# A graph layer on one core: node normalisation moved to ScalarE and h split in PSUM, with another order of issue at the head

## The chip, the core and the metric

The kernel runs on one core of one Trainium2 chip. The metric is the device time of one execution in microseconds: for the kernel before it is 5291.49 us, the median of three runs from 5287.43 to 5294.71.

Engines are called by the profile's names: PE (TensorE matmuls; PEld its weight loads), DVE (VectorE), ACT (ScalarE), POOL (GpSimd) and SP (SyncE, which here only issues DMAs). Each engine works through its own queue in order.

## What is computed

One message passing layer with 12500 nodes of 128 features and 412500 edges, of which the destinations are sorted:

```python
h = jnp.maximum(_layernorm(x, axis=-1), 0.0)
h = h @ W_in2f                                              # per node
Wij = ssp(f_ij @ W_f1 + b_f1) @ W_f2 + b_f2                 # per edge, from 20 numbers
x_ij = h[idx_j] * (Wij * rcut_ij[:, None])                  # per edge
agg = jax.ops.segment_sum(x_ij, idx_i, num_segments=12500)  # idx_i = src, idx_j = dst
out = x + ssp(agg @ W_o1 + b_o1) @ W_o2 + b_o2
```

`ssp(x)` is softplus(x) - log 2; `_layernorm` subtracts the mean of a row and divides by the root of its variance plus 1e-5. All arrays are float32.

## The kernel before

**Nodes.** The nodes are taken in 25 quads of up to four tiles of 128 (`QT` = 4, `NQ` = 25; the last quad has two tiles). `make_h(q)` is a generator: each `yield` ends a stage, and the caller decides when the next stage is issued. The stages are: load `xb`; mean and variance on DVE (`bn_stats`, `bn_aggr`) and `rs`, the reciprocal root, as exp(-0.5 ln(v)) on ACT; a correction step for `rs` on DVE, and on DVE the normalised `xb` = (x - mean) rs (L354); transposes on PE into PSUM (`xps`) and their relu on ACT (`xT`); the product with `win` on PE into PSUM (`hps`) and its rounding to bf16 on ACT (`hb[..., 0, :]`, L367); the rest `left` = hps - hb0 on DVE (L370), and its rounding on ACT (L371); the third part on DVE (L373), and the stores of the three bf16 parts into HBM on SP (L379, L388). `h3_t` is a list of overlapping tables of h, one for each neighbourhood of nodes, so that the rows for a chunk of sorted edges lie in one table.

**Edges.** They are taken in 806 chunks of 512 (`CH`), four chunks to a `Group`. For each chunk:
- `rows`: SP reads a start row from `shifts` and asks for 32 rows of h (`near`).
- `hidden`, `hidden_log`, `hidden_end`, for two chunks at a time: PE makes `z` (PSUM), ACT takes abs, exp and ln (L700, L701, L703), DVE adds (`r`, L709).
- `window`: DVE makes the one-hot `at` from `rel`; `pick`: PE multiplies it with `near` into `picked` (PSUM); `picked`: ACT scales it by the edge weight into `hg` (L822, four instructions).
- `bias`: ACT fills `v` in PSUM with the bias of the second layer (L793); `value`: PE adds r times `wf2` to it (L801).
- `message`: DVE copies the place (L829) and multiplies `v` with `hg` (`o`, L830), and POOL scatters its four tiles into HBM with four indirect DMAs (L834), each to the row in `slot`.
- `columns` (`edges` and `starts`), `blocks`, `rank` and `rank_end` find that row: for each edge the block of 128 source nodes, and by a running count in the PSUM bank `free` the next free slot of that block. `edges` and `starts` work for up to eight groups at once.

`step(k)` issues in this order: groups and rows ahead of time, the message of chunk k, the rest of the last rank, `picked` and `value` of chunk k+1, `pick` and `bias` of chunk k+2, the window of k+3, the end of the hidden layer, blocks, ranks, logs, and `hidden` of chunk k+4. `part(name, upto, make)` issues all chunks up to `upto` that are not yet issued.

**Around it.** The slots are cleared by SP from a tile `zero` (L1218); `zeros` spreads these DMAs over the steps, from step `t0` on. In every step from the sixth on `side()` advances the quads 2 to 24 by one stage, a new quad each nine steps, so the node work ends at step 213 (1352 us); it also checks the ranges of `dst`. After each of seven segments of chunks, `Collect` reads the slots back, compares their places (`to`) and sums them on PE into `agg`; the first of these starts at 2223 us. From step `XK` = 300 on `x_ahead` loads 14 quads of x early and adds the output bias `bo2` to them on DVE (`x_bias`, L426); others follow at the end on POOL. `finish` applies the last two layers.

**Tiles in PSUM.** `acc` (one bank) is shared by `xps`, `hps` and the sums, `v` (three banks) by `v` and `picked`, `z` has two, `free` one, and `count_ps`, which holds the numbers 0 to 127 in each partition, is a tile of its own in a last one.

**The head.** Before the first step the calls at the end of the kernel issue the first stages of quad 0 between the first chunk's work by hand: `h` is the list of the generators of quads 0 and 1, `next(h[0])` advances quad 0.

Of the kernel before, what the change touches and what calls it, by code (L numbers as in the profile page):

```python
# [9 lines left out]
F32 = mybir.dt.float32  # L10
# [7 lines left out]
P = 128  # L18
# [25 lines left out]
def gnn_kernel(  # L44
# [76 lines left out]
    def spread(t, n):  # L121
        return t[:, None, :].to_broadcast([t.shape[0], n, P])
# [204 lines left out]
    def make_h(q, psum):  # L327
# [9 lines left out]
        for i in range(n):  # L337
# [7 lines left out]

        ve = ln.tile([P, QT], F32, name="ve")
        nc.vector.tensor_scalar(ve[:, :n], mv[:, :n, 1], EPS, -0.5, op0=ALU.add, op1=ALU.mult)
        r2 = ln.tile([P, QT], F32, name="r2")
# [3 lines left out]
                                       op0=ALU.add, op1=ALU.mult)  # L352
        for i in range(n):
            nc.vector.tensor_scalar(xb[:, i, :], xb[:, i, :], mv[:, i, 0:1], rs[:, i:i + 1],  # L354
                                    op0=ALU.subtract, op1=ALU.mult)
# [10 lines left out]
        hb = ln.tile([P, QT, 3, P], BF16, name="hb")  # L366
        nc.scalar.activation(hb[:, :n, 0, :], hps[:, :n, :], AF.Copy)  # L367
        yield
        left = ln.tile([P, QT, P], F32, name="left")
        nc.vector.tensor_sub(left[:, :n, :], hps[:, :n, :], hb[:, :n, 0, :])  # L370
        nc.scalar.activation(hb[:, :n, 1, :], left[:, :n, :], AF.Copy)  # L371
        yield
        nc.vector.tensor_sub(hb[:, :n, 2, :], left[:, :n, :], hb[:, :n, 1, :])  # L373
        for (b, rows), table in zip(tables, h3_t):
# [47 lines left out]

    def x_bias(xo, pieces, engine=nc.vector):
        for p, cs, rows in pieces:
            xi = xo[:p, cs, :]
            engine.tensor_add(xi, xi, spread(bo2[:p, :], xi.shape[1]))  # L426

# [110 lines left out]
    with tc.tile_pool(name="edge", bufs=2) as edge, tc.tile_pool(  # L538
# [10 lines left out]

        count_ps = state_ps.tile([P, P], F32, name="count_ps")  # L550

# [42 lines left out]
        class Group:  # L594
# [45 lines left out]
            def columns(self):  # L640
                self.edges()
                self.starts()

            def edges(self):
                if len(self.cols) == 3:
                    w, src_i, _ = self.cols
                    part = edge.tile([P, SB * TG], I32, name="part")
                    nc.vector.tensor_scalar(part[:, :w], src_i[:, :w], 7, None,
                                            op0=ALU.logical_shift_right)
                    blk = edge.tile([P, SB * TG], F32, name="blk")  # L650
                    nc.vector.tensor_copy(blk[:, :w], part[:, :w])
                    nc.vector.tensor_scalar(src_i[:, :w], src_i[:, :w], P - 1, None,
                                            op0=ALU.bitwise_and)
                    place = edge.tile([P, SB * TG], F32, name="place")
                    nc.vector.tensor_copy(place[:, :w], src_i[:, :w])
                    self.cols += [blk, place]
                self.rcut, self.blk, self.place = (t[:, self.at] for t in self.cols[2:5])

            def starts(self):
                if len(self.cols) == 5:  # L660
                    w, blk = self.cols[0], self.cols[3]
                    seg = self.seg
# [15 lines left out]
                    for t, half in ((1, -1.0), (2, 0.0)):  # L678
# [3 lines left out]
                                            seg.T * P - 1.0, None, op0=ALU.add)  # L682
                    self.cols += [start]
                self.start = self.cols[5][:, self.at]

# [103 lines left out]
            def bias(self, c):  # L789


                v = psum.tile([P, QT, P], F32, name="v", bufs=3)
                nc.scalar.activation(v, spread(bf12, QT), AF.Copy)  # L793
                return v
# [184 lines left out]
        def group(j):  # L979
            if j not in groups and j < NG:  # L980
                groups[j] = Group(j)
# [11 lines left out]
        def step(k, units=()):  # L993
# [12 lines left out]
            def message(k):  # L1006
# [96 lines left out]

        def x_ahead(homes, engine):

            pending = []
            for q, xo in homes:
                n = min(QT, NTILE - q * QT)
                pieces = x_pieces(q * QT, n)
                x_load(xo, pieces)  # L1110
                xs[q] = xo
                pending.append((xo, pieces))
                yield
                yield
                if len(pending) > 2:
                    x_bias(*pending.pop(0), engine)
            for w in pending:
                yield
                x_bias(*w, engine)

# [30 lines left out]
        def rest():  # L1151
# [15 lines left out]
            yield from ranges(psum)  # L1167
            late_biases(psum)

        def side():  # L1170
# [12 lines left out]
        with tc.manual_schedule():  # L1183
# [157 lines left out]
```

## Time and profile before

| | |
|---|---|
| median of three runs | 5291.49 us |
| the profiled run | 5291.49 us |
| its span, first to last instruction | 5289.7 us |
| first message `o` starts | 22.27 us |
| first scatter starts | 23.26 us |
| last stage of the last quad (stores on SP) | 1349 to 1352 us |
| early additions to x (L426) | 1920.8 to 2061.7 us, 14 of 677 ns (median) |
| first read of slots | 2223.2 us |
| last scatter starts | 5158.9 us |
| PE clock granted, mean | 0.760 |

The profile is one execution. A group's line has the source line, engine, operation, what it writes and reads with their shapes, how often (x); then the busy time in us, the mean in ns of one, and how long the engine idled just before, with what ended that. Busy time of a group counts overlapping instructions of one engine once. In a timeline the first two numbers are start and duration in us; rows that follow each other are merged (x4), and brackets give the idle time before and what ended it. "issue" is a wait that the profile can't explain, "remote" one ended by a semaphore of which the profile has no instruction. SPq rows are DMA issues on SP's queue. A table of stretches gives for each the busy time and count, the granted clock, the DMA engines' busy share and GB/s.

### The profile page before, as it was taken

How to read it: one execution, taken by the hardware profiler on the slowest of the kernel's cores; microseconds unless marked ns; L12 is line 12 of the kernel's file. 1: busy time of each engine (PE TensorE's matmuls, PEld its weight loads, DVE VectorE, ACT ScalarE, POOL GpSimd, SP SyncE). 2: the span in 40 equal slices, each digit the busy share in tenths (PEclk: the TensorE clock that was granted, in tenths of full speed). 3: DMA queues.
4: the chain of work that ended last, by engine and by line, in shares of the span. 5: the costliest groups of instructions: out<-in, count | busy, mean ns of one | idle time of the engine just before them, and what ended most of it. 6: DMA issues, size and time to landing. Idle time of an engine off the chain costs nothing. (4 is left out here: it accounts for less than half of the span.)

```text
span 5289.7 us, 74340 instructions
## 1 busy us (share of the span) xinstructions
PE 3721.0 (70%) x21594; PEld 2858.0 (54%) x21594; DVE 3142.9 (59%) x7101; ACT 2785.5 (53%) x5466; POOL 3137.3 (59%) x3292
## 2 busy tenths in 40 slices
PE   5565655555665555688888887777787787777778
PEld 4344434334443333466666666666666666666667
DVE  5555555554444454566666666566666666666667
ACT  5555555555555555555555555455554454554443
POOL 5666666656666666666665565555555565555552
PEclk7666666666666666688888878888888888888889
DMA  4545445444333334465666555556555665565547
GB/s 139 155 135 158 143 137 150 126 138 132 109 101 99 97 111 135 132 181 179 179 180 206 175 167 171 153 169 206 173 165 168 191 191 150 170 192 160 152 134 195
DMA packets 515221, 820.65 MB, mean 155 GB/s; under 512 B 177188, under 2 KB 312728, under 8 KB 514812
## 3 DMA queue, kind: packets, MB, share of 16 engines
q1 hardware_dynamic: 411212, 602.55, 40.3%
q0 software_dynamic: 103168, 213.15, 12.1%
q8 instruction: 180, 2.95, 0.2%
q14 instruction: 229, 1.88, 0.1%
q10 hardware_dynamic: 432, 0.13, 0.0%
HBM read 419.75 MB, written 395.69 MB: 154 GB/s over the span
## 5 line engine op out<-in xcount | busy, mean ns | idle before, releaser
L834 POOL DMA_INDIRECT slots<-o,slot x3224 | 3099.7, 961 | 2056.3 <-DVE o L830 1161.4
L822 ACT ACTIVATE hg<-picked,rcut 128x128 f32<-128x128 f32 x3224 | 912.3, 365 | 1400.0 <-remote 716.5
L907 PEld LDWEIGHTS acc<-to,m 128*128 128x128 f32 x8152 | 1210.2, 230 | 478.2 <-issue 338.1
L907 PE MATMUL acc<-to,m 128*128 128x128 f32 x8152 | 1303.7, 321 | 209.0 <-issue 130.4
L801 PEld LDWEIGHTS v<-wf,r 128*128 128x128 f32 x6448 | 1082.8, 249 | 384.7 <-issue 264.4
L801 PE MATMUL v<-wf,r 128*128 128x128 f32 x6448 | 1176.6, 338 | 120.9 <-issue 75.4
L830 DVE TENSOR_TENSOR o<-v,hg 128x512 f32<-128x512 f32 x806 | 552.4, 685 | 967.4 <-remote 469.5
L691 PE MATMUL z<-f,wf 20*128 20x512 f32 x1612 | 635.3, 861 | 468.8 <-DVE r L709 264.4
L886 DVE TENSOR_TENSOR to<-count_ps,m 128x640 f32<-128x640 f32 (+3 forms) x793 | 637.3, 826 | 283.2 <-remote 98.3
L738 DVE TENSOR_REDUCE top<-free 128x4 f32<-128x392 f32 x806 | 448.2, 556 | 446.9 <-remote 286.1
L793 ACT ACTIVATE v<-bf 128x512 f32<-128x512 f32 x806 | 486.0, 603 | 419.3 <-DVE o L830 244.5
L812 PE MATMUL picked<-near,at 96*128 96x128 bf16 x3224 | 389.7, 255 | 394.4 <-DVE o L830 280.0
L709 DVE SCALAR_TENSOR_TENSOR r<-z,nbf,a 128x1024 f32<-128x1024 f32 x403 | 513.9, 1275 | 95.6 <-issue 50.5
L700 ACT ACTIVATE a<-z,bf 128x1024 f32<-128x1024 f32 x403 | 445.0, 1104 | 221.4 <-remote 79.1
L766 PE MATMUL free<-inb,rest_of 128*128 128x392 f16 x806 | 328.0, 407 | 332.0 <-issue 214.7
L812 PEld LDWEIGHTS <-at 96*128 96x128 bf16 x3224 | 309.5, 117 | 453.0 <-issue 428.1
L691 PEld LDWEIGHTS z<-f,wf 20*128 20x128 f32 x1612 | 157.8, 233 | 679.9 <-DVE r L709 353.9
L703 ACT ACTIVATE a<-a,half 128x1024 f32<-128x1024 f32 x403 | 462.7, 1148 | 13.1
L714 DVE TENSOR_TENSOR inb<-count_ps,blk 128x392 f16<-128x392 f32 x806 | 445.3, 553 | 0.0
L701 ACT ACTIVATE a<-a 128x1024 f32<-128x1024 f32 x403 | 425.9, 1057 | 12.8
L733 PE MATMUL free<-inb,after 128*128 128x392 f16 x806 | 329.4, 409 | 9.6 <-issue 6.6
L785 DVE TENSOR_SCALAR at<-rel,prow 96x512 bf16<-96x512 bf16 x806 | 283.5, 352 | 0.0
(113 smaller groups left out, 1227.9 us busy)
## 6 DMA issues: line engine op xcount, KB each, us to landing
m<-slots SPq DMA_DIRECT2D x307, 387.0 KB
m<-slots SPq DMA_DIRECT2D x278, 322.5 KB
rel<-rel_d SPq DMA_DIRECT2D x202, 384.0 KB
slots<-o,slot POOLq DMA_INDIRECT x3224
m<-slots SPq DMA_DIRECT2D x193, 258.0 KB
slots<-zero SPq DMA_DIRECT2D x96, 387.0 KB
f<-in_f_t SPq DMA_DIRECT2D x404, 80.0 KB
slots<-zero SPq DMA_DIRECT2D x58, 516.0 KB
```

The lines of the kernel that those rows point to most:

```text
L691: mm = nc.tensor.matmul(z[:, k, :], wf1[rows, :], self.f[rows, :], start=True, stop=True)
L703: nc.scalar.activation(a, a, AF.Ln, bias=half, scale=0.5)
L709: nc.vector.scalar_tensor_tensor(r, z, nbf1, a, op0=ALU.max, op1=ALU.add)
L738: nc.vector.tensor_reduce(self.top[:, c * QT:(c + 1) * QT], free_v, axis=mybir.AxisListType.X, op=ALU.max)
L793: nc.scalar.activation(v, spread(bf12, QT), AF.Copy)
L801: mm = nc.tensor.matmul(v[:, i, :], r[:, i * P:(i + 1) * P], wf2, start=False, stop=True, skip_group_check=True)
L812: mm = nc.tensor.matmul(ps[:, i, :], at[:, i * P:(i + 1) * P], near, start=i == 0, stop=i == QT - 1, skip_group_check=True)
L822: nc.scalar.activation(hg[:, i, :], ps[:, i, :], AF.Copy, scale=self.rcut[:, j:j + 1])
L830: nc.vector.tensor_mul(o[:, :, :P], v, hg)
L834: put = nc.gpsimd.indirect_dma_start(out=views[j % VIEWS], out_offset=bass.IndirectOffsetOnAxis(ap=self.slot[:, j:j + 1], axis=0), in_=o[: ...
L886: nc.vector.tensor_tensor(to[:, :n, :], count_ps[:, None, :].to_broadcast([P, n, P]), m[:, :n, P:].to_broadcast([P, n, P]), op=ALU.is_equal)
L907: nc.tensor.matmul(self.acc[b // QT][:, i, :], m[:, j, :P], to[:, j, :], start=t == 0, stop=t == self.seg.tiles(b) - 1)
```

## The change

For quads 2 to 24 the mean is subtracted on ACT, with the negative mean `nm` as bias; the factor `rs`, which is positive and so passes through the relu, is applied when h is rounded: four instructions on ACT in place of one, and four on DVE in place of one. For all quads the rest is kept in `hps` in PSUM, so the tile `left` is gone as a step of the split. The early additions to x read the bias from PSUM (`bo2_ps`, beside `count_ps` in one tile), filled once by ACT. The bias of the first two chunks is made by PE with a one-row matmul. The order at the head differs: `edges` and `starts` are one function, the calls before the first step stand in another order, rows for the first steps are asked for later, `hidden` of chunk 2 is issued a step earlier, the message of chunk 1 stands at its place in step 1 instead of in step 0, and the clears begin at step 0 instead of 8.

```diff
 def make_h(q, psum):
         ve = ln.tile([P, QT], F32, name="ve")
+        if q > 1:
+            nm = ln.tile([P, QT], F32, name="nm")
+            nc.vector.tensor_scalar(nm[:, :n], mv[:, :n, 0], -1.0, None, op0=ALU.mult)
+            for i in range(n):
+                nc.scalar.activation(xb[:, i, :], xb[:, i, :], AF.Identity, bias=nm[:, i:i + 1])
...
-        for i in range(n):
+        for i in range(n if q < 2 else 0):
             nc.vector.tensor_scalar(xb[:, i, :], xb[:, i, :], mv[:, i, 0:1], rs[:, i:i + 1],
                                     op0=ALU.subtract, op1=ALU.mult)
...
-        nc.scalar.activation(hb[:, :n, 0, :], hps[:, :n, :], AF.Copy)
+        if q < 2:
+            nc.scalar.activation(hb[:, :n, 0, :], hps[:, :n, :], AF.Copy)
+            yield
+            nc.vector.tensor_sub(hps[:, :n, :], hps[:, :n, :], hb[:, :n, 0, :])
+        else:
+            for i in range(n):
+                nc.scalar.activation(hb[:, i, 0, :], hps[:, i, :], AF.Copy, scale=rs[:, i:i + 1])
+            yield
+            for i in range(n):
+                nc.vector.scalar_tensor_tensor(hps[:, i, :], hps[:, i, :], rs[:, i:i + 1],
+                                               hb[:, i, 0, :], op0=ALU.mult, op1=ALU.subtract)
+        nc.scalar.activation(hb[:, :n, 1, :], hps[:, :n, :], AF.Copy)
         yield
-        left = ln.tile([P, QT, P], F32, name="left")
-        nc.vector.tensor_sub(left[:, :n, :], hps[:, :n, :], hb[:, :n, 0, :])
-        nc.scalar.activation(hb[:, :n, 1, :], left[:, :n, :], AF.Copy)
-        yield
-        nc.vector.tensor_sub(hb[:, :n, 2, :], left[:, :n, :], hb[:, :n, 1, :])
+        nc.vector.tensor_sub(hb[:, :n, 2, :], hps[:, :n, :], hb[:, :n, 1, :])
...
-        count_ps = state_ps.tile([P, P], F32, name="count_ps")
+        numbers = state_ps.tile([P, CH], F32, name="numbers")
+        count_ps, bo2_ps = numbers[:, :P], numbers[:, P:2 * P]
...
 class Group, bias(self, c):
-                nc.scalar.activation(v, spread(bf12, QT), AF.Copy)
+                if self.g * NCHUNK + c < 2:
+                    nc.tensor.matmul(v.rearrange("p t f -> p (t f)"),
+                                     ones[0:1, :].to_broadcast([1, P]), spread(bf12[0:1, :], QT),
+                                     start=True, stop=False, skip_group_check=True)
+                else:
+                    nc.scalar.activation(v, spread(bf12, QT), AF.Copy)
...
 def step(k, units=()):
-            for j in range(max(groups) + 1, min(k + LG, 2 * k + 8) // NCHUNK + 1):
-                group(j)
-            part("rows", min(k + LW, 2 * k + 5, NEXT if k < NEXT - 3 else NCH), rows)
+            group((k + LG) // NCHUNK)
+            part("rows", min(k + LW, 2 * k + 3, NEXT if k < NEXT - 3 else NCH), rows)
...
-            if k in vs:
-                message(k)
+            if has(k):
+                g, c = of(k)
+                g.message(c, vs.pop(k), hgs.pop(k))
...
-            if k:
-                part("end", min(k + LZ - 2, made.get("log", -1)), pairs(hidden_end))
+            part("end", min(k + LZ - 2, made.get("log", -1)), pairs(hidden_end))
...
-            if not k:
-                message(1)
-                part("end", made["log"] - 1, pairs(hidden_end))
-            part("hidden", k + LZ if k > -2 else 1, pairs(hidden))
+            part("hidden", k + LZ, pairs(hidden))
...
-        t0, i = 8, 0
+        t0, i = 0, 0
...
             late_biases(psum)
+            nc.scalar.activation(bo2_ps, bo2, AF.Copy)
...
             next(h[0])
-            groups[0].edges()
+            part("hidden", 0, hidden)
+            part("blocks", 0, blocks)
             next(h[0])
-            part("hidden", 0, hidden)
-            groups[0].blocks(0)
-            made["blocks"] = 0
+            ready = ranks(0)
+            next(ready)
             next(h[0])
             part("log", 0, hidden_log)
-            next(h[0])
-            part("rows", 3, rows)
-            biases(psum)
-            bs[0] = groups[0].bias(0)
-            ready = ranks(0)
-            next(ready)
-            groups[0].starts()
-            part("end", 0, hidden_end)
-            part("window", 0, window)
             next(ready, None)
             made["rank"] = 0
+            next(h[0])
+            part("rows", 1, rows)
+            biases(psum)
+            part("end", 0, hidden_end)
+            bs[0] = groups[0].bias(0)
             group(1)
             aside = side()
-            x_early = x_ahead(early_homes(), nc.vector)
-            x_late = x_ahead(late_homes(), nc.gpsimd)
+            x_early = x_ahead(early_homes(), nc.vector, bo2_ps)
+            x_late = x_ahead(late_homes(), nc.gpsimd, bo2)
```

`x_bias` and `x_ahead` take the bias to add as a new argument; `blocks` calls `columns`, which does the work of `edges` and `starts` in one.

More of the change, by code (lines that the diff above doesn't have):

```diff
@@ L421, in x_load, with x_bias @@
             nc.sync.dma_start(xo[:p, cs, :], x[rows, :].rearrange("(c p) f -> p c f", p=p))
-    def x_bias(xo, pieces, engine=nc.vector):
+    def x_bias(xo, pieces, engine=nc.vector, b=bo2):
         for p, cs, rows in pieces:
             xi = xo[:p, cs, :]
-            engine.tensor_add(xi, xi, spread(bo2[:p, :], xi.shape[1]))
+            engine.tensor_add(xi, xi, spread(b[:p, :], xi.shape[1]))
     def finish(t0, n, sT, quad, psum, z, xo=None, bank=("v", 3)):
@@ L640, in columns @@
             def columns(self):
-                self.edges()
-                self.starts()
-            def edges(self):
                 if len(self.cols) == 3:
@@ L655, in edges @@
                     nc.vector.tensor_copy(place[:, :w], src_i[:, :w])
[L656 to L661, printed above, removed]
                     seg = self.seg
@@ L682, in starts @@
                                             seg.T * P - 1.0, None, op0=ALU.add)
-                    self.cols += [start]
-                self.start = self.cols[5][:, self.at]
+                    self.cols += [blk, place, start]
+                self.rcut, self.blk, self.place, self.start = (t[:, self.at] for t in self.cols[2:])
             def hidden(self, c):
@@ L998, in has @@
                 return 0 <= j < NCH
-            for j in range(max(groups) + 1, min(k + LG, 2 * k + 8) // NCHUNK + 1):
-                group(j)
-            part("rows", min(k + LW, 2 * k + 5, NEXT if k < NEXT - 3 else NCH), rows)
+            group((k + LG) // NCHUNK)
+            part("rows", min(k + LW, 2 * k + 3, NEXT if k < NEXT - 3 else NCH), rows)
             for c, u in units:
                 c.load(u + AHEAD)
-            def message(k):
+            if has(k):
                 g, c = of(k)
                 g.message(c, vs.pop(k), hgs.pop(k))
-            if k in vs:
-                message(k)
             for r in tops:
@@ L1102, in gnn_kernel, with x_ahead @@
                     break
-        def x_ahead(homes, engine):
+        def x_ahead(homes, engine, b):
             pending = []
@@ L1115, in x_ahead @@
                 if len(pending) > 2:
-                    x_bias(*pending.pop(0), engine)
+                    x_bias(*pending.pop(0), engine, b)
             for w in pending:
                 yield
-                x_bias(*w, engine)
+                x_bias(*w, engine, b)
         def as_quad(t):
```

## The prediction

> **What bounds the kernel now.** I read the page first, then the rate of scatters by stretch of time, then the timeline of one stretch, then the groups of the node work, and last the timeline of the head.
>
> ```profile
> span 5289.7 us, 74340 instructions
> PE 3721.0 (70%) x21594; PEld 2858.0 (54%) x21594; DVE 3142.9 (59%) x7101; ACT 2785.5 (53%) x5466; POOL 3137.3 (59%) x3292
> ...
> L834 POOL DMA_INDIRECT slots<-o,slot x3224 | 3099.7, 961 | 2056.3 <-DVE o L830 1161.4
> ```
>
> No engine is full. POOL's 3224 scatters are four to each of 806 chunks; one takes 961 ns and the next starts 0.30 us after it, so POOL alone would need 4 x 1.26 = 5.04 us for a chunk, 4065 us in all. It also stands idle 1161 us for the messages `o`. So the chain that makes a message (PE, ACT, DVE) falls behind POOL again and again. How much the node work, which the change edits, has to do with that is read from the rate with it (until 1350 us) and without it (after):
>
> ```profile
> 100.00:700.00 600.00, 376.24 (x391) 0.65 0.49 148
> 700.00:1300.00 600.00, 368.67 (x383) 0.66 0.46 135
> 1400.00:1700.00 300.00, 190.60 (x199) 0.63 0.37 102
> 1700.00:2000.00 300.00, 192.19 (x198) 0.64 0.38 109
> ```
>
> The columns are the stretch, its length, POOL's busy time and scatters, clock, DMA share, GB/s. With node work: 774 scatters in 1200 us, 6.20 us a chunk; without: 397 in 600 us, 6.05. A quad of nodes is spread over nine steps, so it costs 9 x 0.156 = 1.41 us now, and the 23 quads from the third on cost 32 us together. That is the size of the stake: whatever is done to this work, little more than 32 us can be won.
>
> ```profile
> 613.73 1.12 ACT L822 ACTIVATE hg<-picked,rcut 128x128 f32<-128x128 f32 x4
> 614.88 0.60 ACT L793 ACTIVATE v<-bf 128x512 f32<-128x512 f32 x1
> 615.41 1.10 ACT L700 ACTIVATE a<-z,bf 128x1024 f32<-128x1024 f32 x1
> 616.54 1.06 ACT L701 ACTIVATE a<-a 128x1024 f32<-128x1024 f32 x1
> 617.63 1.15 ACT L703 ACTIVATE a<-a,half 128x1024 f32<-128x1024 f32 x1
> 618.69 1.12 ACT L822 ACTIVATE hg<-picked,rcut 128x128 f32<-128x128 f32 x4
> ...
> 631.22 1.14 ACT L822 ACTIVATE hg<-picked,rcut 128x128 f32<-128x128 f32 x4 [5.79 <-remote]
> ```
>
> The reader is to see that the chain moves in bursts: ACT runs without a gap for some 12 us, then PE, ACT and DVE all stand for 4 to 10 us, and only POOL goes on. What the halt is the trace does not say. In the bursts ACT is the engine with no gap; per chunk it has 1.12 + 0.60 + half of 3.31 = 3.4 us.
>
> **The node work of quads 3 to 25** (22.5 full quads, the last has two tiles).
>
> ```profile
> L354 DVE TENSOR_SCALAR xb<-xb,mv,rs 128x128 f32<-128x128 f32 x86 | 24.6, 371 | 0.8
> L370 DVE TENSOR_TENSOR left<-hps,hb 128x512 f32<-128x512 f32 x22 | 15.1, 686 | 40.9 <-ACT hb L367 21.2 <-issue 19.7
> L373 DVE TENSOR_TENSOR hb<-left,hb 128x512 bf16<-128x512 f32 x22 | 14.9, 678 | 0.0
> ...
> L371 ACT ACTIVATE hb<-left 128x512 bf16<-128x512 f32 x22 | 13.6, 618 | 2.5 <-DVE inb L714 0.9 <-issue 0.8 <-DVE left L370 0.8
> L367 ACT ACTIVATE hb<-hps 128x512 bf16<-128x512 f32 x22 | 13.0, 590 | 79.1 <-remote 47.0 <-PE hps L365 11.5 <-PE v L801 7.6
> ...
> L342 ACT ACTIVATE rs<-mv,eps 128x4 f32<-128x4 f32 (+1 forms) x22 | 6.4, 290 | 32.0 <-DVE mv L339 14.0 <-DVE st L338 9.1 <-issue 8.9
> ```
>
> ACT gains four 128x128 activations for centring (nearest row L822, 1.13 us for four with their overlap) and has four in place of one for the first part of h: 1.13 - 0.59 = 0.54. Together +1.67 us a quad, 37.6 us in all. DVE loses L354 (24.6 / 21.5 = 1.14 us a quad), gains `nm` (as L347, 0.155), and has four scaled subtractions in place of L370. No row shows DVE writing PSUM; bounds are L370's own 0.69 and four of L354's full durations, 4 x 0.371 = 1.48; I take 1.14, the overlapped four of L354, which also read a per-partition scalar: +0.45. Net -0.53 us a quad, -12.0 us. The second and third parts only change which memory they read: L371 (SBUF) 618 ns against L367 (PSUM) 590, L373 678 against L370 686: nothing. The stages are the same in number, so the SP stores of h stay in their steps.
>
> What a microsecond of this work costs: per quad ACT now has 0.29 + 0.21 + 0.60 + 0.59 + 0.62 = 2.3 us and DVE 4.9 (statistics 1.79, small 0.63, L354 1.14, L370 and L373 1.36). If the 1.41 us are owed to both alike, a microsecond costs 0.195, and the edit (1.67 - 0.53) x 0.195 x 22.5 = +5. If ACT alone sets it, 0.61, and the edit costs 0.61 x 1.67 x 22.5 = +23. If DVE alone, 0.29 x -0.53 x 22.5 = -3. With no cover at all, +38. The row without gaps is ACT's, which speaks for the +23; but POOL is mostly busy in those bursts and the halts follow, which speaks for less. I take +12.
>
> The new wait: ACT's centring waits for `nm` on DVE, at the end of a step; behind it stand the next step's four `hg`, for which DVE's `o` waits, for which POOL waits. L342 waits at the same place of a step already, 32.0 / 22 = 1.45 us; it does so for the statistics, which are over when `nm` is due. I put 0, hidden by PE being later than either; without that cover, 23 x 1.45 = 33 us of ACT at most.
>
> **Scatters beside DVE.** Third parts and early additions of x will have one operand in PSUM.
>
> ```profile
> 54.03 0.68 DVE L373 TENSOR_TENSOR hb<-left,hb 128x512 bf16<-128x512 f32 x1
> 54.03 1.51 POOL L834 DMA_INDIRECT slots<-o,slot  x1 [0.30 <-issue]
> ```
>
> A scatter beside L373 took 1.51 us against the usual 0.96. Such cases are few: between 100 and 1400 us a scatter takes 964 ns, between 1600 and 1900 us 959; 836 x 5 ns = 4 us of POOL, which has idle time. I take -3, bounds 0 and -4. The adds of 14 early quads of x are 0.68 us each from SBUF, as L830 is with PSUM: 0 for DVE. The Trainium skill (SBUF — State Buffer, Who interferes with whom) says that a DVE instruction with two SBUF inputs shuts out a GpSimd one that reads SBUF for its whole length; taken literally for 23 + 14 instructions of 0.68 us that would make 25 us. The mean of the scatters speaks against more than a few of them. Four 128x128 operations take 1.14 us on DVE (L354) and 1.13 on ACT (L822), so only the load of each engine decides. The skill (ScalarE: Activation LUTs, Rules for kernel authors) would keep additions on VectorE, which speaks against the centring; by its figure of up to three times the speed for bf16 the four would be near 0.4 us on DVE, and these fp32 rows don't show that.
>
> **The head.** Its order of issue is another one.
>
> ```profile
> 13.67 0.69 DVE L373 TENSOR_TENSOR hb<-left,hb 128x512 bf16<-128x512 f32 x1 [0.70 <-ACT hb L371]
> ...
> 17.73 3.73 SPq L637 DMA_DIRECT2D near<-h  x4
> ...
> 22.27 0.68 DVE L830 TENSOR_TENSOR o<-v,hg 128x512 f32<-128x512 f32 x1
> ```
>
> Today `starts` (14.60 to 16.81, 2.2 us) and the end of the first rank (18.57 to 19.73, 1.16 us) come after L373. In the changed order both stand before it on DVE: columns to 13.85, blocks to 14.4, subtraction to 15.1, rank to 16.26, L373 to 16.95, against 14.36 now: h's first store is 2.6 us later, and `near` behind it on SP. ACT's log chain, now 13.70 to 17.08, starts after the second part at 15.75: +2.05. The first `o` moves from 22.27 by 2.0 to 2.6; I take +2.3. Rows for two chunks fewer are asked for ahead, so pick(2) waits in its own step for a `near` that stands on SP behind four `f`, three stores and a clear (2.7 + 1.9 + 0.4 us of issue): 0 to +4, I take 0, since o(2) now comes only at 36.93 and waits for PE. Clears begin eight steps earlier: 108 before 1000 us spread over 156 steps instead of 148, so about 5.5 of them in the first 50 us, where the DMA share is 0.47: 0 to +4, taken as 0. The hidden layer of chunk 2 comes earlier, which may give back up to 3. The bias of the first two chunks goes from ACT (0.60) to PE (half of L691's 2.08 us for two, 1.04): 0, while PE waits for `r`; 2.1 us at most. Head: +2.3, from -3 to +10.
>
> Sum: 5289.7 + 12 - 3 + 2.3 = 5301.0; the profiled run is 1.8 us above its span and is the median of the three: **5303**, +0.22%.
>
> **Rivals.**
> *No change*: the halts hide ACT's new work, since ACT idles before L367 (79 us) and L342 (32 us) already; then only head and scatters count, 5289.7 + 2.3 - 3 + 1.8 = 5291. For it: ACT is 57% busy over this stage. Against: no gaps in the bursts.
> *Faster*: DVE's queue is what holds the messages back in this stage, because L354 and L373 sit there between one `o` and the next. If the 32 us are owed to DVE's 4.9 us and the chain of L354 and L373 (1.8 of them) stops counting, 32 x 1.8 / 4.9 = -12; with the scatters and head 5289.7 - 12 - 3 + 2.3 + 1.8 = 5279. It decides if DVE and not ACT is the engine without gaps in the quads' steps. Against: the replaced subtraction gives 0.45 us back, and DVE has gaps of 0.6 us in the burst shown.
> *Much slower*: ACT's work has no cover, +38, with the head's 2.3: 5331. From the point where POOL has no lead over the messages, which its 1161 us of waiting says is often.
>
> **How the numbers follow.** Forecast (slower by 5 to 25 us) 0.37, much slower 0.10, no change 0.28, faster 0.25. A measurement of this kernel tells about 0.2% (10.6 us) from no change. So slower 0.47, same 0.28, faster 0.25. The forecast's own range is 5297 to 5316; to hold 8 in 10 it takes in no change and most of faster below (5279) and half of much slower above (5326).
>
> **What would show it.** Right: the first `o` near 24.5 us; 6.25 us or more a chunk from 100 to 1300 us and 6.05 after; L354's line in ACT's rows at 1.13 us for four; scatters at 960 ns. Wrong: fewer than 6.15 us a chunk in the node stage, or a changed rate after 1400 us, where nothing but the 14 adds differs; or a centring that waits several microseconds for `nm`.

## The result, and the profile after

The changed kernel takes 5324.35 us (median of 22 runs, 5293.22 to 5342.98) against 5293.30 us before (22 runs, 5272.99 to 5312.38) on the same chip. The ratio of the two kernels is 1.0050, with a 95% interval of 1.0035 to 1.0064: slower by 18 to 34 us, about 26 (the two medians alone are 31 apart). The forecast was +11.5 us, with the right sign and less than half of the size.

One caution for all that follows: the profiled execution after, 5293.22 us, is the shortest of its 22 runs. Its loss of 1.8 us of span is not the loss of 26 us in the median, so the profile shows which waits and durations are there, and only the medians of many runs price them. From the page after:

```profile
span 5291.5 us, 74527 instructions
...
PE 3743.6 (71%) x21598; PEld 2857.9 (54%) x21598; DVE 3133.8 (59%) x7101; ACT 2824.6 (53%) x5622; POOL 3140.1 (59%) x3292
...
L843 POOL DMA_INDIRECT slots<-o,slot x3224 | 3102.3, 962 | 2051.1 <-DVE o L839 1158.1
```

ACT has 39 us more work, as costed (37.6), and DVE 9 less (12 were costed). A scatter still takes 962 ns and POOL still waits 1158 us for messages, against 1161. By stretch of time (columns: stretch, length, POOL's busy time and scatters, clock, DMA share, GB/s):

```profile
100.00:700.00 600.00, 369.40 (x383) 0.66 0.49 145
700.00:1300.00 600.00, 367.49 (x384) 0.66 0.45 134
1400.00:1700.00 300.00, 190.63 (x199) 0.64 0.36 101
1700.00:2000.00 300.00, 191.17 (x200) 0.64 0.37 108
```

With node work 767 scatters in 1200 us, 6.26 us a chunk against 6.20; after it 399 in 600 us against 397, no change. So even this short run lost some 11 us (0.06 x 192 chunks) between 100 and 1300 us, and got the like back later, in the collection, where the change does nothing and single runs of either kernel differ by as much. The rows of the edited node work, from the groups between 100 and 1360 us:

```profile
L381 DVE SCALAR_TENSOR_TENSOR hps<-hps,rs,hb 128x128 f32<-128x128 f32 x88 | 31.5, 357 | 57.4 <-ACT hb L378 41.8 <-issue 13.2
L351 ACT ACTIVATE xb<-xb,nm 128x128 f32<-128x128 f32 x90 | 28.6, 387 | 23.9 <-DVE nm L349 14.2 <-issue 5.4 <-DMA slots<-zero 4.3
L378 ACT ACTIVATE hb<-hps,rs 128x128 bf16<-128x128 f32 x88 | 25.0, 366 | 90.5 <-remote 66.5 <-DMA near<-h 10.1 <-PE hps L370 7.0
L385 DVE TENSOR_TENSOR hb<-hps,hb 128x512 bf16<-128x512 f32 x22 | 14.9, 678 | 0.0
```

The reader is to see three things. Four centrings take 28.6 / 22.5 = 1.27 us (1.13 was costed), four scaled roundings 25.0 / 22 = 1.14 (as costed), four scaled subtractions written to PSUM 31.5 / 22 = 1.43 (1.14 was costed, with 1.48 as the bound). DVE now stands 41.8 us for ACT's `hb` at the head of its queue, where it stood 21.2. Most of the difference is not the queue's doing, though: counted in the traces, 28.8 of the 41.8 us fall into the halts, stretches of over 2.5 us in which no instruction of PE, DVE or ACT runs, against 9.0 of the 21.2. Outside the halts it is 13.0 against 12.2 us. And ACT stands 23.9 us before the centring, 14.2 of it for `nm`; the list of waits says how this is spread (total, times, longest):

```profile
ACT xb L351 <- DVE nm L349: 14.2, 5, 4.3
```

Five of 23 quads wait, 2.8 us each, one 4.3, none of it in a halt: what the forecast named as a sign against itself.

The head, by its timeline (start, duration, row, idle time before):

```profile
21.11 2.08 PE L695 MATMUL z<-f,wf 20*128 20x512 f32 x4
...
23.12 2.08 PE L810 MATMUL v<-wf,r 128*128 128x128 f32 x8
...
25.30 0.69 DVE L839 TENSOR_TENSOR o<-v,hg 128x512 f32<-128x512 f32 x1 [2.61 <-PE v L810]
...
33.42 0.61 PE L821 MATMUL picked<-near,at 96*128 96x128 bf16 x4 [3.33 <-DMA near<-h]
34.15 0.53 PE L737 MATMUL free<-inb,after 128*128 128x392 f16 x1
...
34.72 0.57 DVE L742 TENSOR_REDUCE top<-free 128x4 f32<-128x392 f32 x1 [2.49 <-PE free L737]
...
36.45 1.12 DVE L359 TENSOR_SCALAR xb<-xb,mv,rs 128x128 f32<-128x128 f32 x4
...
37.55 0.68 DVE L839 TENSOR_TENSOR o<-v,hg 128x512 f32<-128x512 f32 x1
...
38.51 0.96 POOL L843 DMA_INDIRECT slots<-o,slot  x1 [7.24 <-DVE o L839]
```

The first `o` comes at 25.30, 3.03 later than before: PE now makes the hidden layer of chunk 2 (21.11) ahead of the `v` that this message needs. Then the pick of chunk 2 waits 3.33 us for `near`, with PE standing. Behind it on PE stands the running count `free` (34.15), for which DVE's `top` waits (34.72), and behind that on DVE, after a stage of node work (35.79 to 37.48, its largest part the 36.45 row), the second message (37.55), whose `v` has been ready since 30.1 (28.18 + 1.91 by the row of its matmuls). In the kernel before the same three, the pick, `top` and the message, stood so:

```profile
26.82 0.63 PE L812 MATMUL picked<-near,at 96*128 96x128 bf16 x4
...
28.02 0.57 DVE L738 TENSOR_REDUCE top<-free 128x4 f32<-128x392 f32 x1 [2.54 <-PE v L801]
...
29.16 0.69 DVE L830 TENSOR_TENSOR o<-v,hg 128x512 f32<-128x512 f32 x1
```

The message came at 29.16: 3.03 + 3.33 + 1.7 are 8.1 of its 8.4 us of delay. Its scatters start at 38.51 against 30.1, and by chunk 9 they are 7.8 us late (88.3 against 80.5).

### The profile page after: what moved, and what is told of

The parts are those of the page before. It is cut to its first block, busy times and chain, and to the rows that moved or that the text cites. A ratio compares the mean times of both kernels' runs of the same rounds, so it can differ in the third digit from the quotient of the medians.

```text
span 5291.5 us, 74527 instructions
## 1 busy us (share of the span) xinstructions
PE 3743.6 (71%) x21598; PEld 2857.9 (54%) x21598; DVE 3133.8 (59%) x7101; ACT 2824.6 (53%) x5622; POOL 3140.1 (59%) x3292
## 5 line engine op out<-in xcount | busy, mean ns | idle before, releaser
L895 DVE TENSOR_TENSOR to<-numbers,m 128x640 f32<-128x640 f32 (+3 forms) x793 | 636.2, 826 | 258.4 <-remote 112.5
L704 ACT ACTIVATE a<-z,bf 128x1024 f32<-128x1024 f32 x403 | 445.5, 1105 | 199.7 <-remote 88.3
L718 DVE TENSOR_TENSOR inb<-numbers,blk 128x392 f16<-128x392 f32 x806 | 445.4, 553 | 0.0
```

The costliest lines, as they stand in the source:

```text
L895: nc.vector.tensor_tensor(to[:, :n, :], count_ps[:, None, :].to_broadcast([P, n, P]), m[:, :n, P:].to_broadcast([P, n, P]), op=ALU.is_equal)
```

## Experiments

Twelve kernels, each with a dozen runs beside the kernel before on the same chip. They ran in three sets of four, on three chips, and the kernel before takes 5363.29, 5294.20 and 4227.25 us on them. So ratios are compared inside a set first; across sets only with care, and the third set ran in another regime, as its part below shows.

**The parts of the change alone (e1 to e4).** e1 has the order and asks of the changed head and the bias of two chunks on PE, with node work and additions to x as before; the core of the edit:

```
-            part("rows", min(k + LW, 2 * k + 5, NEXT if k < NEXT - 3 else NCH), rows)
+            part("rows", min(k + LW, 2 * k + 3, NEXT if k < NEXT - 3 else NCH), rows)
...
-        t0, i = 8, 0
+        t0, i = 0, 0
```

> The kernel before with the changed head alone (order of issue, rows asked for later, clears from step 0, PE bias for two chunks); node work and early x as before. The changed kernel is 26 us (0.5%) slower in the median, and in its profile scatter 20 starts 10 us later than before. Theory A, two costs: the head's 10 us stay to the end and the node work has the rest: 5301 to 5306 where before has 5293, ratio 1.0015 to 1.0025. Theory B, the head has it all: ratio 1.004 to 1.006. Theory C, the head's loss is made up later, because POOL waits in every stretch anyway: ratio 0.999 to 1.001.

Measured: 5377.89 us, ratio 1.0027 (1.0009 to 1.0044), +5 to +24 us. Its head, by the timeline:

```profile
25.35 0.69 DVE L826 TENSOR_TENSOR o<-v,hg 128x512 f32<-128x512 f32 x1 [2.58 <-PE v L797]
...
33.23 0.61 PE L808 MATMUL picked<-near,at 96*128 96x128 bf16 x4 [3.09 <-DMA near<-h]
...
38.31 0.95 POOL L830 DMA_INDIRECT slots<-o,slot  x1 [7.00 <-DVE o L826]
```

The same rows as in the whole change, within 0.2 us. Against e3, which has the old head on the same chip, chunk 9's scatters start 8.4 us later and those of chunk 215 5.8 later. In between, at chunks 50 and 100, those of e1 start 0.9 and 4.2 us earlier, so two single profiles do not show whether POOL wins the head's loss back.

e2 has the changed node work of the quads from the third on, and nothing else of the change:

```
+            nm = ln.tile([P, QT], F32, name="nm")
+            nc.vector.tensor_scalar(nm[:, :n], mv[:, :n, 0], -1.0, None, op0=ALU.mult)
+            for i in range(n):
+                nc.scalar.activation(xb[:, i, :], xb[:, i, :], AF.Identity, bias=nm[:, i:i + 1])
...
+                nc.scalar.activation(hb[:, i, 0, :], hps[:, i, :], AF.Copy, scale=rs[:, i:i + 1])
...
+                nc.vector.scalar_tensor_tensor(hps[:, i, :], hps[:, i, :], rs[:, i:i + 1],
+                                               hb[:, i, 0, :], op0=ALU.mult, op1=ALU.subtract)
```

> The kernel before with the changed node work of quads 3 to 25 alone; head and early x as before. Theory A: ratio 1.002 to 1.004 (10 to 20 us), and the scatters of chunks 20 to 215 are spread over 10 to 20 us more. Theory B: 0.999 to 1.001. Theory C: 1.004 to 1.006. The prediction's +12 us would be 1.0023.

Measured: 5386.97 us, ratio 1.0049 (1.0028 to 1.0071), +15 to +38 us. Nearly all of what the whole change costs. Its groups between 100 and 1360 us show both waits again, the one for ACT on DVE (24.6 of its 46.2 us in halts), the one for `nm` on ACT (none in halts):

```profile
L382 DVE SCALAR_TENSOR_TENSOR hps<-hps,rs,hb 128x128 f32<-128x128 f32 x88 | 31.5, 358 | 57.6 <-ACT hb L379 46.2 <-issue 9.1
L351 ACT ACTIVATE xb<-xb,nm 128x128 f32<-128x128 f32 x86 | 27.3, 387 | 30.1 <-DVE nm L349 16.7 <-issue 8.6 <-DVE r L354 4.8
```

e3 has only the 14 early additions to x take the bias from PSUM:

```
-            engine.tensor_add(xi, xi, spread(bo2[:p, :], xi.shape[1]))
+            engine.tensor_add(xi, xi, spread(b[:p, :], xi.shape[1]))
...
+            nc.scalar.activation(bo2_ps, bo2, AF.Copy)
```

> The kernel before with the early additions to x reading the bias from PSUM alone. All theories: no difference, ratio 0.999 to 1.001; 14 additions of 0.67 us. A scatter between 1900 and 2100 us should take 0.96 us where it takes 0.97 before.

Measured: 5368.82 us, ratio 1.0001 (0.9981 to 1.0021): no effect that can be seen. The scatters did get shorter where the additions run (groups between 1950 and 2150 us). In e3:

```profile
L835 POOL DMA_INDIRECT slots<-o,slot x133 | 127.5, 959 | 74.6 <-DVE o L831 37.2 <-issue 36.7 <-DMA slots<-o,slot 0.3
```

and in e1, which adds from SBUF as the kernel before does:

```profile
L830 POOL DMA_INDIRECT slots<-o,slot x131 | 128.5, 981 | 72.7 <-issue 35.7 <-DVE o L826 35.6 <-DMA slots<-o,slot 1.2
```

22 ns a scatter, 133 x 0.022 = 2.9 us of POOL, which idles some 37 us there for messages and had no use for them. The Trainium skill (SBUF — State Buffer, Who interferes with whom) says that a VectorE instruction with two SBUF inputs contends with a GpSimd one that reads SBUF; the direction agrees with these rows, and the price here is nil.

e4 is the whole change on this chip.

> The changed kernel itself on the same chip: ratio 1.0035 to 1.0064 as measured. If the parts add up, its loss is the sum of the losses of the three other runs.

Measured: 5389.86 us, ratio 1.0052 (1.0033 to 1.0071), as on the first chip. The parts add up to 0.27 + 0.49 + 0.01 = 0.77% and the whole is 0.52%; the intervals of the parts are wide enough for that, so whether their losses overlap is left open. The four profiles put the loss into the stage with node work: between 100 and 1300 us POOL issues 763 scatters in e3, 758 in e1, 749 in e2 and 739 in e4 (6.29, 6.33, 6.41 and 6.50 us a chunk), and between 1400 and 2000 us 389, 389, 394 and 387.

**What in the node work costs (e5 to e8).** e5 keeps the scaled split in PSUM and leaves the centring on DVE:

```
-            nc.vector.tensor_scalar(xb[:, i, :], xb[:, i, :], mv[:, i, 0:1], rs[:, i:i + 1],
-                                    op0=ALU.subtract, op1=ALU.mult)
+                nc.vector.tensor_scalar(xb[:, i, :], xb[:, i, :], mv[:, i, 0:1], None,
+                                        op0=ALU.subtract)
```

> The kernel before with the scaled split of h in PSUM alone for quads 3 to 25; the mean is subtracted on DVE as before. ACT gets 0.5 us a quad more and DVE 0.45. The whole node change cost 24 us here (ratio 1.0049). Theory L, ACT's load is what costs: a third of it, ratio 1.001 to 1.002. Theory W, ACT's wait for the mean is what costs: 0.999 to 1.001. Theory S, the split costs (four instructions for one on two engines in turn): 1.004 to 1.006.

Measured: 5317.17 us, ratio 1.0042 (1.0020 to 1.0065). So the split, with the centring left on DVE, costs 11 to 34 us. Its groups between 100 and 1360 us:

```profile
L381 DVE SCALAR_TENSOR_TENSOR hps<-hps,rs,hb 128x128 f32<-128x128 f32 x88 | 31.5, 358 | 53.6 <-ACT hb L378 27.3 <-issue 24.0
...
L355 DVE TENSOR_SCALAR xb<-xb,mv 128x128 f32<-128x128 f32 x86 | 19.2, 308 | 0.0
```

DVE waits 53.6 us at the subtraction where it waited 40.9 (for ACT 27.3 against 21.2, and outside the halts 14.4 against 12.2), and the subtraction is 16.4 us longer in all (31.5 against 15.1); the centring without its factor is 5.4 shorter (19.2 against 24.6).

e6 is the kernel before with four ScalarE operations a quad more, of the centring's size, that wait for nothing and that nobody reads:

```
+            idle = ln.tile([P, QT, P], F32, name="idle", bufs=1)
+            for i in range(n):
+                nc.scalar.activation(idle[:, i, :], ident, AF.Identity, bias=eps)
```

> The kernel before with four ACT instructions of 128x128 more in each quad from the third on, which read constants, wait for nothing and whose result nobody reads: 1.27 us of ACT a quad, 29 us in all. Theory L: ratio 1.003 to 1.005, most of what the node change costs. Theories W and S: 0.999 to 1.001.

Measured: 5291.50 us, ratio 0.9993 (0.9976 to 1.0010). Between 100 and 1360 us:

```profile
L347 ACT ACTIVATE idle<-ident,eps 128x128 f32<-128x128 f32 x86 | 27.2, 386 | 0.0
...
L374 DVE TENSOR_TENSOR left<-hps,hb 128x512 f32<-128x512 f32 x22 | 15.1, 685 | 43.2 <-ACT hb L371 23.2 <-issue 20.1
```

27 us more of ACT, none of it waiting, and the time does not move (-13 to +5 us); DVE's wait for `hb` stays as before (23.2 against 21.2). This is the clearest answer of the study: the load of ScalarE by itself, at this place in its queue, is not the price.

e7 is e2 with `nm` made a stage earlier, so that the centring waits for nothing:

```
+            nm = ln.tile([P, QT], F32, name="nm")
+            nc.vector.tensor_scalar(nm[:, :n], mv[:, :n, 0], -1.0, None, op0=ALU.mult)
         rs = ln.tile([P, QT], F32, name="rs")
```

> The kernel before with the changed node work, but the negative mean is made on DVE a stage earlier, right after the statistics, so that the centring on ACT waits for nothing; as much work as in the node change alone. Theory W: the loss shrinks from 24 us to under 8, ratio under 1.0015, and ACT idles under 5 us before the centring instead of 30. Theories L and S: ratio 1.004 to 1.006 as with the wait.

Measured: 5305.28 us, ratio 1.0019 (1.0000 to 1.0038).

```profile
L383 DVE SCALAR_TENSOR_TENSOR hps<-hps,rs,hb 128x128 f32<-128x128 f32 x90 | 32.2, 358 | 68.9 <-ACT hb L380 48.7 <-issue 17.8
L352 ACT ACTIVATE xb<-xb,nm 128x128 f32<-128x128 f32 x86 | 27.2, 385 | 0.0
```

The wait for `nm` is gone (0.0 us) and +11 us remain (0 to +20), with the subtraction's wait for ACT as long as ever. By the medians e7 is 12 us cheaper than e5 on the same chip, so the centring on ACT, with no wait, does not look dearer than on DVE; their intervals overlap. With the wait, in e2, the whole cost +24 on another chip. That the wait is worth the difference of 13 us is possible, but not shown: the intervals of e2 and e7 overlap too.

e8 moves the relu of `xT` from ACT to DVE, in quads of the same range:

```
-        nc.scalar.activation(xT[:, :n, :], xps[:, :n, :], AF.Relu)
+            nc.vector.tensor_scalar(xT[:, :n, :], xps[:, :n, :], 0.0, None, op0=ALU.max)
```

> The kernel before with the relu of the transposed nodes on DVE instead of ACT from the third quad on: ACT loses 0.6 us a quad and its in-order wait for PE's transposes (104 us of ACT's idle time at this line), DVE gets both. Theory L: 0.997 to 0.999. Theory W says that it matters which engine waits in order: if ACT is the engine to keep free, 0.996 to 0.999; if DVE is, 1.001 to 1.004. Theory S: no difference, 0.999 to 1.001.

Measured: 5308.03 us, ratio 1.0022 (1.0005 to 1.0039).

```profile
L362 DVE TENSOR_SCALAR xT<-xps 128x512 f32<-128x512 f32 x21 | 14.5, 692 | 99.6 <-remote 57.0 <-PE xps L359 20.9 <-PE v L804 13.7
```

ACT is rid of 12.4 us of work, DVE has 14.5 more and waits 99.6 us with that instruction at the head of its queue: slower by 3 to 21 us. With e6 this points to DVE's side as the place where node work costs. Whether by the instruction's own time or by the wait in front of it, these rows do not tell. Neither does it alone: e2 gives DVE 5 us less of node work between 100 and 1360 us (centring -24.6, `nm` +3.5, subtraction +16.4) and is slower; and e7, whose wait for `hb` outside the halts is the longest of the three (28.4 us, against 21.6 in e2 and 14.4 in e5), costs the least of them.

In this set, too, the loss is in the stage with node work: between 100 and 1300 us POOL issues 772 scatters in e6, 768 in e8, 763 in e7 and 759 in e5: the fewer, the slower, but for e7 and e8, whose times differ by 3 us.

**Load or wait, and a candidate (e9 to e12).** The last set was to separate the two and to try the reverse of the change's effect: DVE relieved and nothing made to wait.

e9 is the kernel before with four DVE operations of the centring's form more a quad, which wait for nothing and which nobody reads:

```
+            for i in range(n):
+                nc.vector.tensor_scalar(idle[:, i, :], ident, mv[:, i, 0:1], rs[:, i:i + 1],
+                                        op0=ALU.subtract, op1=ALU.mult)
```

> The kernel before with four DVE operations of 128x128 more in each quad from the third on (L354's own form, on a constant, read by nobody, waiting for nothing): 1.14 us of DVE a quad, 26 us in all, the mirror of the four idle ones on ScalarE (e6), which cost nothing. Theory D-load (a microsecond of DVE in a quad's steps delays the messages, waiting or not): ratio 1.002 to 1.004, 6.24 us a chunk or more between 100 and 1300 us. Theory D-wait (only an instruction that waits at the head of DVE's queue for ScalarE costs; work that waits for nothing falls into DVE's gaps as it does on ScalarE): 0.9985 to 1.001. The prediction's price for DVE's load (0.195 us for each us, 22.5 quads): +5 us, 1.001.

e10 makes the first part of h by four ScalarE copies in place of one, which was to let DVE wait longer with no more to do:

```
+            for i in range(n):
+                nc.scalar.activation(hb[:, i, 0, :], hps[:, i, :], AF.Identity, bias=0.0)
```

> The kernel before with the first part of h made by four ScalarE copies of a tile each in place of one (0.59 to 1.13 us a quad); the subtraction stays one DVE instruction, unscaled. DVE's work is the same, only its wait for ScalarE at L370 gets longer, from 21 us to about 33 us between 100 and 1360 us. D-wait: 1.002 to 1.004, most of what the split alone cost (1.0042). D-load: 0.999 to 1.001, since DVE has nothing more to do and ScalarE's load was free in e6; the cost of the split then lies in the four scaled subtractions.

e11 has the whole normalisation on ScalarE, in a step of its own, so that it waits for nothing:

```
+            nc.vector.scalar_tensor_tensor(nm[:, :n], mv[:, :n, 0], -1.0, rs[:, :n],
+                                           op0=ALU.mult, op1=ALU.mult)
+            yield
+            for i in range(n):
+                nc.scalar.activation(xb[:, i, :], xb[:, i, :], AF.Identity,
+                                     scale=rs[:, i:i + 1], bias=nm[:, i:i + 1])
```

> The kernel before with the whole normalisation of quads 3 to 25 on ScalarE (scale 1/s, bias -m/s), in a step of its own after both are ready, so that it waits for nothing; the load of x is asked for one step less ahead so that the quad takes as many steps. DVE is rid of L354 (1.14 us a quad) for one 128x4 operation (0.16), ScalarE gains 1.13 us. D-load: faster, -0.98 us of DVE a quad, 0.997 to 0.999. D-wait: 0.999 to 1.001, since L354 waits for nothing today (0.8 us idle before it). ScalarE's load as the price: slower, 1.002 or more. A candidate for the best kernel.

Measured, beside 4227.25 us (33 runs) of the kernel before: e9 4229.27 (1.0005, 0.9996 to 1.0014), e10 4225.12 (0.9996, 0.9987 to 1.0005), e11 4228.88 (1.0003, 0.9994 to 1.0012). By the letter of the expectations e9 falls to the theory of waits and e10 to that of load, which exclude each other. Neither may be read so, since the chip of this set runs the kernel in another regime. e9's POOL by stretch, and two lines of its list of waits (total, times, longest):

```profile
100.00:700.00 600.00, 456.70 (x471) 0.70 0.61 183
700.00:1300.00 600.00, 455.77 (x474) 0.68 0.52 150
```

```profile
POOL slots L839 <- issue: 770.2, 2526, 0.3
...
POOL slots L839 <- DVE o L835: 46.8, 73, 19.6
```

945 scatters in 1200 us are 5.08 us a chunk, all but the 5.04 that POOL needs by itself. POOL waits 47 us for messages in all, where it waited 1161; what is left is the 0.30 us between its scatters. Here the messages are hardly ever late, so nothing that is done to the node work can show: e9's 22.6 us of idle DVE work in the quads between 100 and 1000 us, e10's longer rounding and e11's relief of DVE alike. (In e10 the four copies took 0.77 us a quad and not 1.13, and DVE's wait for `hb` did not get longer: 5.6 us between 100 and 1000 us, against 6.7 in e9.) The rows of e9 and of e11, from their groups in that stretch:

```profile
L374 DVE TENSOR_SCALAR idle<-ident,mv,rs 128x128 f32<-128x128 f32 x80 | 22.6, 352 | 0.0
```

```profile
L363 ACT ACTIVATE xb<-xb,nm,rs 128x128 f32<-128x128 f32 x80 | 32.7, 478 | 0.0
```

e11, the candidate, beats nothing here, and whether it would where messages are late was not tried. (With both a factor and an offset per partition the operation takes 478 ns, with the offset alone 385: 1.63 us a quad, not the 1.13 of its expectation.)

e12 is e1 with the rows asked for as early as before, and with the line of `step` that issues the groups as it was before:

```
-            part("rows", min(k + LW, 2 * k + 3, NEXT if k < NEXT - 3 else NCH), rows)
+            part("rows", min(k + LW, 2 * k + 5, NEXT if k < NEXT - 3 else NCH), rows)
...
-            part("rows", 1, rows)
+            part("rows", 3, rows)
```

> e1_head (the head of the changed kernel alone, 1.0027) with its rows asked for as early as in the kernel before, and all else of the changed head left (order of the first steps, clears from the start, bias of two chunks on TensorE). If the late rows (pick of chunk 2 waiting 3.3 us for near) are what the head costs beyond the 3 us of the first message: ratio 1.0005 to 1.0015, the scatters of chunk 9 at +3 to +4 us against +8. If the order and the clears cost it: 1.002 to 1.003 and chunk 9 still at +7 or more.

Measured: 4232.80 us, ratio 1.0012 (1.0003 to 1.0021), 1 to 9 us.

```profile
29.91 0.63 PE L808 MATMUL picked<-near,at 96*128 96x128 bf16 x4
...
30.58 1.14 ACT L818 ACTIVATE hg<-picked,rcut 128x128 f32<-128x128 f32 x4 [1.82 <-PE picked L808]
...
36.13 0.96 POOL L830 DMA_INDIRECT slots<-o,slot  x1 [4.85 <-DVE o L826]
```

The pick of chunk 2 has no wait and comes 3.3 us earlier than in e1 (33.23), the second chunk's scatters 2.2 earlier (36.13 against 38.31). Chunk 9 is 2.3 to 4.4 us later than in e9 to e11, which have the old head, against 8.4 for e1 beside e3. So the late rows, with the groups, make about half of what the head loses by then, and the late first `v`, with the order around it, the rest. It does not last in the profile: the scatters of chunk 215 start at 1123.5 us, between those of e9 to e11 (1122.7 to 1124.0). That profile is of the shortest of e12's runs; what makes the median longer it does not show. The ratio of e1 itself on this chip was not taken.

## Why the forecast was right in sign and short in size

**What bounds the kernel.** Held for this chip: POOL waits 1158 us for messages, and of the stretches forecast only the one with node work changed its rate (6.26 us a chunk; 6.25 or more was forecast, and no change after 1400 us). It does not hold for every chip, as the last set shows. That no more than 32 us can be won was not put to a test.

**The node work, put at +12.** Measured alone at +24 to +26 us (e2). ACT's operations were sized well, +1.82 us a quad (1.27 + 1.14 - 0.59) against +1.67; DVE's relief came out at half, -0.24 (0.16 + 1.43 - 0.69 - 1.14) against -0.53, because the scaled subtractions stand near the bound of 1.48. The step that failed is the price, "The row without gaps is ACT's, which speaks for the +23". It took an engine that looks busy in a burst for the one that sets the pace. At 0.61 us for each us e6 should have cost 17 us (0.61 x 1.27 x 22.5), 1.0032, and its interval ends at 1.0010. The price between the two ends came out low, and for a reason that was not the cause: 27 us of ACT's load cost 5 us at most, while the split, with 0.55 us a quad more of ACT, costs 11 to 34 us. What e5 has and e6 has not is more of DVE: the subtraction 0.74 us a quad longer, and 53.6 us of standing in front of it against 43.2. e8 agrees. What of this is the price stays open: e9 and e10 ran where neither work nor waiting counts, DVE's node work as a whole got less in e2 and in the changed kernel, and its wait for `hb` outside the halts is no longer in the changed kernel than before (13.0 against 12.2 us). That the split is four instructions in place of one on two engines in turn is a third possibility, which no run separates. That the rest `hps` stays in its PSUM bank a stage longer does not show at the transposes that next need the bank: PE idles 0.0 us before them in e5 as before.

**The new wait, put at 0.** Wrong as the forecast itself defined it. "I put 0, hidden by PE being later than either": ACT stands 24 to 30 us in front of the centring (after, e2), near the 33 given as the bound. The row used for it, L342's wait for the statistics, was of the right size (1.45 us a quad); it should have been charged a second time and not been taken as cover. In time it may be worth some 13 us by e2 and e7, if the two chips may be compared; their intervals overlap.

**Scatters, put at -3.** The interval of e3 (-10 to +11 us) holds it and zero. Scatters became shorter as said; POOL had no use for it.

**The head, put at +2.3, bounds -3 and +10.** Mis-sized: e1 gives +14.6 (5 to 24), and the profiles 8 us by chunk 9. The first `o` was forecast 2.0 to 2.6 later and came 3.03 later; DVE's order was followed, PE's was not, where the hidden layer of chunk 2 (2.08 us) now stands ahead of the first `v`. The pick of chunk 2, "0 to +4, I take 0, since o(2) now comes only at 36.93 and waits for PE", waited 3.33 us: it looked at the message of chunk 2, while the one that pays is the message of chunk 1, by way of `free` and `top`, which stand behind the pick. And a step was not costed at all: that message moves from the end of step 0 into step 1, behind a stage of node work (1.7 us). How much of this lasts to the end is not shown: e1's median is 14.6 us longer, but in the profiles of e1 and e3 the gap comes and goes, and in e12's it is gone by chunk 215.

**The sum.** Two terms were short, by about 12 each, and e1 and e2 together come out above the whole. The sign was right partly by luck: what spoke for it was ACT's load, and the load of ACT is the part that costs little or nothing. The measured 5324 us lies above the forecast's own 5297 to 5316 and just inside the wider range that was to hold 8 in 10. The rival "no change" falls by the interval; "faster" by e2, and e7 shows nothing won either. Its idea that DVE's queue holds the messages fits e5, e6 and e8; but DVE had 9 us less to do and the kernel was slower, so DVE's load alone does not give the time. "Much slower" (+38 with no cover) is refuted for load by e6.

## What to carry to other kernels

Before you price moved work by the engine whose rows have no gaps, load that engine alone with operations that wait for nothing: here 27 us of it cost 5 us at most, and a busy-looking engine was not the pace-maker. For each edit, ask how long its instruction will stand at the head of its queue for another engine, and do not put a new wait at nothing because an old one stands at the same place: ACT stood 24 to 30 us before the centring. But before you take a longer wait in a row for the cause, take off what falls into halts that hit whatever instruction is next: here that was 28.8 of 41.8 us, and the rest had not grown. For a changed order at the start, follow the first three messages through every engine's queue, not only the first one: the first came 3.0 us later, the second 8.4.

## What the runs showed of the hardware

The chip, or what else differed between the three sets, makes more difference than any edit. The same kernel before took 5363, 5294 and 4227 us on the three chips. Durations of single operations are the same: a scatter 961 and 963 ns, four `hg` 1.12 and 1.13 us. On the slower chips there are stretches in which no instruction of PE, DVE or ACT runs: counted in the traces, those over 2.5 us are 73 and 296 us together in the kernel before, 71 and 281 us in e5, but 5 and 16 us in e9, 3 and 10 us in e10 on the fast chip. They are less than a third of the 1066 us between these chips. SP's register operations, which the views leave out, differ in the same way: of 3228 in a run, 394 in the kernel before and 399 in e5 take over 0.4 us, mostly about 0.70, where 0.04 is usual; in e9 and e10 none takes over 0.19. The mean granted clock differs too, 0.760 against 0.825 to 0.830, but in the node stage only from 0.65 to 0.70, which does not make 5.08 out of 6.20 us a chunk while POOL, ACT and DVE need no less for each operation. What ends many of the waits in these stretches the trace calls "remote"; their cause was not found. On the chips with many of them the runs of one kernel spread over 39 us (5273 to 5312, the kernel before), on the other over 12 (4220 to 4232), so that on the former one profile can't show a cost of 10 us.

Two durations that no row before could give: a scaled subtraction of 128x128 on DVE, from PSUM to PSUM, 357 ns, and 1.43 us for four; a ScalarE operation of that size 366 to 387 ns with one value per partition, and 478 with two.
